# Sparse graph attention on one core: k and v rows of every batch stored in the original order by GpSimd, without a table of places

## The chip, the core and the metric

The kernel runs on one core of a Trainium2 chip. The metric is the device time of one execution in microseconds (us); three executions of the kernel before gave 1935.06, 1941.86 and 1942.67. One more execution was taken by the hardware profiler.

## What is computed

For 16 batches of 1024 rows with 512 numbers each, the reference is one layer of masked attention with eight heads, a residual and a normalisation of each row:

```
q, k, v = x @ Wq + bq, x @ Wk + bk, x @ Wv + bv      # 8 heads of 64
scores  = q . k / 8 + (1 - adj) * -1e9               # adj: 1024 x 1024, of 0 and 1
out     = softmax(scores) @ v
result  = layernorm(x + out @ Wo + bo)
```

The matrix adj is the same for all batches and is sparse: entry (i, j) is 1 with probability min(1, w_i w_j / 256), where w falls as one over the square root of the row number. Rows with a small number have up to some 80 keys, most have few, some none (such a row attends to all keys equally).

## The kernel before, in words

**Ranks.** The kernel sorts the rows by their number of keys, on the chip. `ranks` loads adj in eight tiles of 128 rows. For each, `most` (L382) counts the keys of each row on ScalarE (ACT), in place, and lets VectorE (DVE) multiply the tile by the column numbers and search the eight greatest, which are the row's last eight keys. From count and row number a key is made; TensorE (PE) spreads the keys over all partitions, and DVE compares each row's key with all others (L421), which gives its rank. GpSimd (POOL) scatters row number, count and keys by rank into a table `order` in device memory, and SP loads it back in sorted order as `ranked`; its first column, as integers, is `asked_row`: which row stands at each place of the sorted order. From then on x of batches 1 to 15 is gathered by POOL in sorted order, eight tiles of 128 rows a batch.

**Projections.** `transpose_x` and `pair` do a batch's tiles two by two: transposes, q, k and v (k and v of a pair by seven products of blocks in place of eight). k and v of 128 rows lie side by side in a tile `kv` of 128 x 1024 numbers (a pool of five buffers), and `send` stores it to `kv_rows`, a table of 1025 rows of 4 KB in device memory with three versions in turn (b % 3). q goes to `q_rows`. The last row of `kv_rows` serves queries without keys: zeros for k, the mean of all v.

**Attention by gathers.** A tile of 128 sorted queries works on blocks: block i is the i-th key of each of its queries, a gather of 128 rows from `kv_rows` by POOL (`gather`, L960). Seven tiles have 28 such blocks, and the two with most keys have six more, in which 128 edges are listed with their queries, which are gathered as well. So a batch has 34 blocks and 40 gathers for them. DVE multiplies q and k (`products`, L996) and adds by heads (`scores`), ACT takes the exponential, ACT or DVE weighs v, DVE adds up, or PE sums the edges.

**Row numbers.** Batch 0 is projected before the ranks are known, so its rows lie in the original order and the gathers use `key_row0`, the key's own number. The rows of later batches lie in sorted order, and the gathers use `key_row`, the key's place. The places come from a table `place_of`: seven small DVE operations (L438 to L443) turn ranks into places, SP stores 1024 numbers of 4 bytes (L444), and `places` (L475) has POOL fetch, 128 numbers at a time, the place of each key: 35 gathers.

**Order of the work.** The program is written out step by step: step n, from -39 to 543 and beyond, holds the exponentials of block n + 3, the products and scores of block n + 4, the gathers up to block n + 8, and a number of PE units (projections, output products) by a running credit. Each engine runs its own instructions in this order, so one that waits holds up all behind it on its engine. `later(k, ...)` puts a function k steps ahead. Steps below 0 are the lead-in: ranks, the projections of batch 0 and part of batch 1, and the lists of edges (`edges(7)` from step -24, `edges(6)` from step -9). Projections run one to two batches ahead of the attention.

**What the steps of the prediction touch.** DVE's column search is L384 and L385, the combinations T1 and T2 of the weights, which PE needs for its first seven-product pair, L333 and L334. `out_q` (L674) takes a buffer of the pool `q` of two; the tile `zero` (L305) is a third user of this pool. POOL's instructions of a batch are gathers of k and v (L986), of edge queries (L956), of x for the projections and for the residual (both L819, tiles `x` and `y`), the scatter of the result (L892), one gather of v (L966) and a power for each tile's variance (L880), whose result DVE uses two steps later (L883). SP stores kv (L692) and q, and loads q.

Of the kernel before, what the change touches and what calls it, by code (L numbers as in the profile page):

```python
# [10 lines left out]
F32 = mybir.dt.float32  # L11
# [31 lines left out]
ROWS = 3  # L43
# [11 lines left out]
PLACES_FROM = -22  # L55
# [112 lines left out]
def kernel(  # L168
# [75 lines left out]
    with ExitStack() as main:  # L244
# [34 lines left out]
        key_row, key_row0 = (one.tile([P, NS + NK], I32, name=name) for name in ("key_row", "key_row0"))  # L279
# [10 lines left out]
        place_row = one.tile([P, NT], I32, name="place_row")  # L290
        key, rank, moved = (one.tile([P, NT], F32, name=name) for name in ("key", "rank", "moved"))
# [7 lines left out]
        place_of = dram.tile([N + 1, 1], I32, name="place_of")  # L299
# [5 lines left out]
        zero = work.tile([1, D], F32, tag="q", name="zero", bufs=2)  # L305
        nc.gpsimd.memset(zero, 0.0)
# [5 lines left out]
        def loads():  # L312

            load_w(W["q"], wq)
            broadcast(bq_bc, bq)
            nc.vector.tensor_scalar(bq_bc, bq_bc, scale, None, op0=OP.mult)
            yield

            B12[0] = work.tile([P, 2, D], F32, tag="kv", name="b12", bufs=5)
            load_w(B11, wk[0:HD2, :])  # L320
            load_w(B21, wk[HD2:D, :])
            load_w(B12[0], wv[0:HD2, :])
            load_w(B22, wv[HD2:D, :])
            for _ in range(5):
                yield
            load_w(W["o"], wo)
            for i in range(ROWS):
                nc.scalar.dma_start(kv_rows[i][N:N + 1, 0:D], zero)
# [5 lines left out]
            nc.vector.tensor_tensor(T2, B22, T1, op=OP.subtract)  # L334
# [39 lines left out]
        def later(k, fn):  # L374
            plan.setdefault(now[0] + k, []).append(fn)
# [6 lines left out]
        def most(t, scratch):  # L382
            nc.scalar.activation(ADJ[t], ADJ[t], AF.Copy, accum_out=asked[:, t, 1:2])
            nc.vector.tensor_tensor(scratch, ADJ[t], place, op=OP.mult)  # L384
            nc.vector.max(out=asked[:, t, 2:], in_=scratch)  # L385

        def ranks():
# [6 lines left out]
            last_place = small.tile([1, 1], I32, name="last_place", bufs=1)  # L394
            nc.gpsimd.iota(last_place, pattern=[[1, 1]], base=N, channel_multiplier=0)
            nc.gpsimd.dma_start(place_of[N:N + 1, :], last_place)
            keys = work.tile([P, N], F32, tag="kv", name="keys", bufs=5)
            while now[0] <= max(ADJ_AT):
                for t in ADJ_AT.get(now[0], ()):
                    most(t, keys)  # L400
                yield
# [7 lines left out]
            row = work.tile([P, N], F32, tag="kv", name="key_of", bufs=5)  # L409
# [48 lines left out]
            for tiles, K in ((slice(0, short), SHORT_KEYS), *((slice(t, t + 1), OWN[t]) for t in range(short, NT))):  # L458
                n = tiles.stop - tiles.start
                rows, at = ranked[:, tiles, 2:2 + K], own[tiles.start]  # L460
                missing = absent[:, at:at + n * K].rearrange("p (t k) -> p t k", t=n)
                nc.vector.tensor_scalar(missing, rows, 0.0, None, op0=OP.is_lt)
                nc.vector.scalar_tensor_tensor(
                    key_row0[:, NS + at:NS + at + n * K].rearrange("p (t k) -> p t k", t=n), missing, NO_ROW, rows,
                    op0=OP.mult, op1=OP.max,
                )
            nc.vector.tensor_scalar(absent, absent, -NEG, None, op0=OP.mult)
            nc.vector.tensor_copy(key_row[:, NS:], key_row0[:, NS:])
# [28 lines left out]
        def edges(t):  # L497
# [60 lines left out]
            for i0 in range(0, nb, step):  # L558
# [19 lines left out]
                for rows in (key_row0, key_row):  # L578
                    nc.vector.tensor_tensor(rows[:, g0:g0 + n], e[:, 1, :], e[:, 0, :], op=OP.max)
# [12 lines left out]
            preps.append(places(range(first[t], first[t] + nb), 1))  # L592
# [72 lines left out]
        def pair(b, j):  # L665
# [8 lines left out]
            def out_q(i, p):  # L674

                assert gathered[0] >= NBT * (b - ROWS + 1)
                q = work.tile([P, D], F32, tag="q", name=f"q_{b}_{tt[i]}", bufs=2)
                nc.vector.scalar_tensor_tensor(q, p, scale, bq_bc, op0=OP.mult, op1=OP.add)
                later(1, lambda: nc.sync.dma_start(q_rows[b % ROWS][ds(tt[i] * P, P), :], q))
# [272 lines left out]
        def keys_of(b):  # L952
            return key_row if b else key_row0

# [5 lines left out]
        def gather(n):  # L960
            b, t, i = blocks[n]
            assert i < OWN[t] or t in listed
            if (t, i) == (ONE_KEY_AT[0], 0):
# [4 lines left out]
                    in_offset=bass.IndirectOffsetOnAxis(ap=keys_of(b)[:, g:g + 1], axis=0), element_offset=D,  # L968
# [10 lines left out]
            else:  # L979
# [8 lines left out]
                in_offset=bass.IndirectOffsetOnAxis(ap=keys_of(b)[:, g:g + 1], axis=0),  # L988
# [189 lines left out]
        prep.setdefault(PLACES_FROM, []).append(places([NS + own[t] + i for t in range(NT) for i in range(OWN[t])], 3))  # L1178
# [130 lines left out]
```

## Time and profile before

| | |
|---|---|
| three executions | 1935.06, 1941.86, 1942.67 us |
| profiled execution: its time | 1968.62 us |
| its span, first to last instruction | 1966.8 us |
| mean granted clock of PE | 0.984 of full speed |
| busy | PE 1874.8, DVE 1729.9, ACT 1549.2, POOL 1284.7 us |
| DMA | 541 MB in 185298 packets, 0.82 of 16 engines busy |
| PE busy in the first 165 us | 124.88 us |
| PE busy from 165 to 1500 us | 1325.55 of 1335 us |
| PE busy from 1500 us to the end | 424.33 of 467 us |

An engine's idle time is told with what ended it: "5.67 <-DVE t L334" means 5.67 us without work until the DVE instruction of line 334 that writes t was done. In groups of instructions the columns are line, engine, operation, tiles, form and count, then busy time and mean duration in ns of one, then the idle time before them. In tables by stretch each engine has its busy time and number of instructions; the last three columns are PE's granted clock, the busy share of the 16 DMA engines, and GB/s. POOL's durations are rough; its starts are not.

### The profile page before, as it was taken

The page shows a single profiled execution, that of the slowest core. Times are in us where ns is not written, and L with a number is a line of the kernel's source. Part 1 is how long each engine was busy: PE and PEld are TensorE (multiplying, and loading weights), DVE is VectorE, ACT ScalarE, POOL GpSimd, SP SyncE. Part 2 cuts the span into 40 slices and gives each one's busy share as a digit, 9 for nine tenths or more (in the row PEclk, how much of TensorE's full clock was granted, in tenths as well). Part 3 has the DMA queues.
Part 4 walks back from the last instruction along what each step waited for, and adds up shares of the span by engine and source line. Part 5 has one row for each costly group of instructions (what it writes and reads, how often), then busy time and mean ns, then how long its engine had stood idle before and what let it go on. Part 6 is the DMA issues. An engine that isn't in the chain of part 4 may idle for free.

```text
span 1966.8 us, 25244 instructions
## 1 busy us (share of the span) xinstructions
PE 1874.8 (95%) x5259; PEld 907.2 (46%) x5259; DVE 1729.9 (88%) x3506; ACT 1549.2 (79%) x6072; POOL 1284.7 (65%) x1201
## 2 busy tenths in 40 slices
PE   7959999999999999999999999999999999899996
PEld 3424444444545445454545445444544444344443
DVE  5658889999999998999998989989999898999894
ACT  3515777988888888888888888788879888989794
POOL 1455566777666676776777676666767676666684
PEclk9979999999999999999999999999999999999998
DMA  7427778898889888887988888887988889998983
GB/s 263 88 73 241 239 262 275 271 325 278 310 265 308 275 285 277 294 315 247 321 265 308 269 283 284 278 293 251 315 290 307 285 295 331 335 353 273 353 294 136
DMA packets 185298, 541.44 MB, mean 275 GB/s; under 512 B 32975, under 2 KB 32987, under 8 KB 185134
## 3 DMA queue, kind: packets, MB, share of 16 engines
q0 software_dynamic: 118736, 388.89, 60.4%
q1 hardware_dynamic: 63504, 145.33, 20.4%
q10 hardware_dynamic: 2894, 5.52, 0.8%
q14 instruction: 120, 0.98, 0.2%
q8 instruction: 44, 0.72, 0.1%
HBM read 423.95 MB, written 140.37 MB: 287 GB/s over the span
## 4 chain that ended last, share of the span: by engine, by line
PE 73%; DVE 11%; issue 4%; DMA 4%; ACT 2%; POOL 1%; another core or an unknown queue 1%; SPq 0%; POOLq 0%; DVEq 0%
PE po L648 19%; PE pq L648 15%; PE pp L765 12%; PE z L765 9%; PE x L765 8%; DVE qk L1007 2%; PE poT L1090 2%; PE pxT L615 2%; PE sum L1056 2%; PE sum L1057 2%; DVE s L1011 2%; ACT pv L1031 1%; DVE pv L1047 1%; DMA codes<-in_adj_dram,asked_row 1%; DMA kvg<-kv_rows,key_row 1%
## 5 line engine op out<-in xcount | busy, mean ns | idle before, releaser
L1031 ACT ACTIVATE pv<-kvg,pv 128x64 f32<-128x64 f32 x3544 | 892.5, 339 | 0.6 <-ACT pv L1021 0.6
L986 POOL DMA_INDIRECT kvg<-kv_rows,key_row x544 | 618.4, 1137 | 329.7 <-ACT pv L1031 96.8
L648 PE MATMUL po<-wo,oT 128*128 128x512 f32 x944 | 437.7, 597 | 2.0 <-DVE y L866 1.1
L648 PE MATMUL pq<-wq,xT 128*128 128x512 f32 x904 | 426.1, 601 | 1.0 <-DVE found L518 1.0
L1011 DVE TENSOR_REDUCE s<-qk 128x8 f32<-128x512 f32 x544 | 370.6, 681 | 7.4
L1007 DVE TENSOR_TENSOR qk<-qt,kvg 128x512 f32<-128x512 f32 x448 | 306.7, 684 | 9.3 <-DMA kvg<-kv_rows,key_row 8.6
L648 PEld LDWEIGHTS po<-wo,oT 128*128 128x128 f32 x944 | 177.7, 192 | 198.7 <-issue 188.3
L648 PEld LDWEIGHTS pq<-wq,xT 128*128 128x128 f32 x904 | 170.4, 193 | 198.3 <-issue 183.8
L765 PE MATMUL pp<-t,s 128*128 128x512 f32 x504 | 241.1, 602 | 12.2 <-DVE t L334 5.7
L765 PE MATMUL x<-b,xT 128*128 128x512 f32 x504 | 237.9, 595 | 0.0
L1047 DVE TENSOR_TENSOR pv<-pv,pv 128x520 f32<-128x520 f32 x336 | 233.4, 695 | 2.4 <-ACT pv L1031 1.7
L1021 ACT ACTIVATE pv<-s,absent 128x8 f32<-128x8 f32 x448 | 130.2, 293 | 69.7 <-DVE s L1011 53.3
L819 POOL DMA_INDIRECT x<-in_x_dram,asked_row x120 | 131.3, 1094 | 71.2 <-PE pxT L615 41.5
L892 POOL DMA_INDIRECT out_dram<-y,asked_row x128 | 151.5, 1183 | 37.9 <-issue 25.2
L658 ACT ACTIVATE sq_k<-kv 128x128 f32<-128x128 f32 x512 | 150.8, 300 | 13.8 <-issue 8.5
L765 PEld LDWEIGHTS pp<-t,s 128*128 128x128 f32 x504 | 95.5, 193 | 124.4 <-issue 116.6
L765 PEld LDWEIGHTS x<-b,xT 128*128 128x128 f32 x504 | 95.4, 191 | 114.0 <-issue 111.3
L956 POOL DMA_INDIRECT qg<-q_rows,query_row x96 | 106.3, 1108 | 51.0 <-issue 24.5
L765 PE MATMUL z<-b,s 128*128 128x512 f32 x252 | 122.8, 611 | 17.4 <-DVE kv L793 17.4
L819 POOL DMA_INDIRECT y<-in_x_dram,asked_row x102 | 115.1, 1129 | 30.7 <-issue 29.8
L765 PE MATMUL z<-t,s 128*128 128x512 f32 x252 | 119.8, 599 | 0.0
L765 PE MATMUL pp<-t,xT 128*128 128x512 f32 x252 | 118.5, 593 | 0.0
(208 smaller groups left out, 2582.0 us busy)
## 6 DMA issues: line engine op xcount, KB each, us to landing
kv_rows<-kv SPq DMA_DIRECT2D x128, 512.0 KB
q_rows<-q SPq DMA_DIRECT2D x113, 256.0 KB
qt<-q_rows SPq DMA_DIRECT2D x105, 256.0 KB
kvg<-kv_rows,key_row POOLq DMA_INDIRECT x544
residual<-x SPq DMA_DIRECT2D x26, 256.0 KB
y<-residual SPq DMA_DIRECT2D x26, 256.0 KB
adj<-in_adj_dram POOLq DMA_DIRECT2D x8, 512.0 KB
spill<-oT SPq DMA_DIRECT2D x10, 256.0 KB
```

Of the source, the lines that this page charges most:

```text
L648: nc.tensor.matmul(p, lhs(c), w[:, c, :], start=(c == 0), stop=(c == NPAIR - 1))
L658: nc.scalar.activation(sq, s[:, ts(h, P)], AF.Square, scale=scale, accum_out=sums[:, h:h + 1])
L765: nc.tensor.matmul(R[bank], l[:, ts(c, P)], right[:, c, :], start=(first and c == 0), stop=(c == 1), skip_group_check=True,)
L819: nc.gpsimd.indirect_dma_start(out=y, out_offset=None, in_=x_rows, in_offset=bass.IndirectOffsetOnAxis(ap=asked_row[:, t:t + 1], axis=0), ...
L892: nc.gpsimd.indirect_dma_start(out=out_rows[b, t], out_offset=bass.IndirectOffsetOnAxis(ap=asked_row[:, t:t + 1], axis=0), in_=y, in_offse ...
L956: nc.gpsimd.indirect_dma_start(out=q, out_offset=None, in_=q_rows[b % ROWS], in_offset=bass.IndirectOffsetOnAxis(ap=rows, axis=0))
L986: nc.gpsimd.indirect_dma_start(out=KG[n], out_offset=None, in_=kv_rows[b % ROWS], in_offset=bass.IndirectOffsetOnAxis(ap=keys_of(b)[:, g:g ...
L1007: nc.vector.tensor_tensor(QK[n], q, KG[n][:, 0:D], op=OP.mult)
L1011: nc.vector.tensor_reduce(S[n], QK.pop(n).rearrange("p (h d) -> p h d", d=HD), axis=AX.X, op=OP.add)
L1021: nc.scalar.activation(PV[n][:, D:], S.pop(n), AF.Exp, bias=bias)
L1031: nc.scalar.activation(pv[:, ts(h, HD)], v[:, ds(D + h * HD, HD)], AF.Copy, scale=pv[:, D + h:D + h + 1])
L1047: nc.vector.tensor_tensor(PV[b, t], PV[b, t], pv, op=OP.add)
```

## The change

The rows of `kv_rows` are kept in the original order in all batches. For batches 1 to 15 the tile kv, which holds rows in sorted order, is scattered by row number from POOL, two steps after it is ready instead of one, through eight views of `kv_rows` that are declared disjoint, so that the eight scatters of a batch do not wait for each other. Batch 0 is stored by SP as before. Keys need no translation: `key_row0`, `place_of`, `places`, its 35 gathers, the seven DVE operations and SP's store go.

In `most` DVE now reads the tile of adj as loaded, ahead of ACT, which writes its copy to another tile. The tile `zero` goes (the zeros come from `zeros`), and the first two q tiles of batch 0 take buffers of the pool `y` of six.

The core of the diff:

```diff
-        def most(t, scratch):
-            nc.scalar.activation(ADJ[t], ADJ[t], AF.Copy, accum_out=asked[:, t, 1:2])
+        def most(t, scratch, copied):
             nc.vector.tensor_tensor(scratch, ADJ[t], place, op=OP.mult)
             nc.vector.max(out=asked[:, t, 2:], in_=scratch)
+            nc.scalar.activation(copied, ADJ[t], AF.Copy, accum_out=asked[:, t, 1:2])
...
-            for at, by in ((LONE, LONE), (LONE + P, -LONE - P), (2 * P, P)):
-                nc.vector.tensor_scalar(key, rank, float(at), float(by), op0=OP.is_ge, op1=OP.mult)
-                if at == LONE:
-                    nc.vector.tensor_copy(moved, key)
-                else:
-                    nc.vector.tensor_tensor(moved, moved, key, op=OP.add)
-            nc.vector.tensor_tensor(place_row, rank, moved, op=OP.add)
-            nc.sync.dma_start(place_of[0:N, :].rearrange("(t p) o -> p (t o)", p=P), place_row)
...
-        def places(columns, per_step):
-
-            for i, g in enumerate(columns):
-                nc.gpsimd.indirect_dma_start(
-                    out=key_row[:, g:g + 1], out_offset=None, in_=place_of,
-                    in_offset=bass.IndirectOffsetOnAxis(ap=key_row0[:, g:g + 1], axis=0), bounds_check=N, oob_is_err=False,
-                )
-                if i % per_step == per_step - 1:
-                    yield
...
-                q = work.tile([P, D], F32, tag="q", name=f"q_{b}_{tt[i]}", bufs=2)
+                tag, bufs = ("q", 2) if b or j else ("y", Y_BUFS)
+                q = work.tile([P, D], F32, tag=tag, name=f"q_{b}_{tt[i]}", bufs=bufs)
...
             def send(i):
                 kv = KV[b, tt[i]]
-                later(1, lambda: nc.sync.dma_start(kv_rows[b % ROWS][ds(tt[i] * P, P), :], kv))
+                if b:
+                    later(2, lambda: nc.gpsimd.indirect_dma_start(
+                        out=kv_views[b % ROWS][tt[i]], out_offset=bass.IndirectOffsetOnAxis(ap=asked_row[:, tt[i]:tt[i] + 1], axis=0),
+                        in_=kv, in_offset=None,
+                    ))
+                else:
+                    later(1, lambda: nc.sync.dma_start(kv_rows[0][ds(tt[i] * P, P), :], kv))
...
-                in_offset=bass.IndirectOffsetOnAxis(ap=keys_of(b)[:, g:g + 1], axis=0),
+                in_offset=bass.IndirectOffsetOnAxis(ap=key_row[:, g:g + 1], axis=0),
```

More of the change, by code (lines that the diff above doesn't have):

```diff
@@ L54 @@
 REST_FROM = {7: -24, 6: -9}
-PLACES_FROM = -22
 PRODUCT = 0.86
@@ L278 @@
         sums = one.tile([P, NS, P], F32, name="sums")
-        key_row, key_row0 = (one.tile([P, NS + NK], I32, name=name) for name in ("key_row", "key_row0"))
+        key_row = one.tile([P, NS + NK], I32, name="key_row")
         query_row, query_row0 = (one.tile([P, NS], I32, name=name) for name in ("query_row", "query_row0"))
@@ L289 @@
         asked, ranked = (one.tile([P, NT, 2 + TOP], F32, name=name) for name in ("asked", "ranked"))
-        place_row = one.tile([P, NT], I32, name="place_row")
-        key, rank, moved = (one.tile([P, NT], F32, name=name) for name in ("key", "rank", "moved"))
+        key, rank = (one.tile([P, NT], F32, name=name) for name in ("key", "rank"))
         rank_row, asked_row = (one.tile([P, NT], I32, name=name) for name in ("rank_row", "asked_row"))
@@ L298 @@
         order = dram.tile([N, 2 + TOP], F32, name="order")
-        place_of = dram.tile([N + 1, 1], I32, name="place_of")
+        kv_views = [dram_disjoint_views(rows, NT) for rows in kv_rows]
         order_views = dram_disjoint_views(order, NT)
@@ L304 @@
         residual = [dram.tile([P, D], F32, name=f"residual_{i}") for i in range(B * NT - SPILL[0])]
-        zero = work.tile([1, D], F32, tag="q", name="zero", bufs=2)
-        nc.gpsimd.memset(zero, 0.0)
         zeros = work.tile([P, D + HEADS], F32, tag="pv0", name="zeros", bufs=3)
@@ L327, in loads @@
             for i in range(ROWS):
-                nc.scalar.dma_start(kv_rows[i][N:N + 1, 0:D], zero)
+                nc.scalar.dma_start(kv_rows[i][N:N + 1, 0:D], zeros[0:1, 0:D])
                 if i:
@@ L393, in ranks @@
             nc.vector.tensor_copy(asked[:, :, 0], query)
[L394 to L397, printed above, removed]
+            keys, row = (work.tile([P, N], F32, tag="kv", name=name, bufs=5) for name in ("keys", "key_of"))
             while now[0] <= max(ADJ_AT):
                 for t in ADJ_AT.get(now[0], ()):
-                    most(t, keys)
+                    most(t, keys, row)
                 yield
@@ L408, in ranks @@
                 nc.tensor.matmul(pk[t // 4][:, ts(t % 4, P)], keys[:, ts(t, P)], ident, start=True, stop=True)
-            row = work.tile([P, N], F32, tag="kv", name="key_of", bufs=5)
             for i in range(2):
@@ L463, in ranks @@
                 nc.vector.scalar_tensor_tensor(
-                    key_row0[:, NS + at:NS + at + n * K].rearrange("p (t k) -> p t k", t=n), missing, NO_ROW, rows,
+                    key_row[:, NS + at:NS + at + n * K].rearrange("p (t k) -> p t k", t=n), missing, NO_ROW, rows,
                     op0=OP.mult, op1=OP.max,
@@ L467, in ranks @@
             nc.vector.tensor_scalar(absent, absent, -NEG, None, op0=OP.mult)
-            nc.vector.tensor_copy(key_row[:, NS:], key_row0[:, NS:])
             for t in SHORT:
@@ L577, in edges @@
                 nc.vector.tensor_scalar(e[:, 0, :], e[:, 1, :], 0.0, NO_ROW, op0=OP.is_lt, op1=OP.mult)
-                for rows in (key_row0, key_row):
-                    nc.vector.tensor_tensor(rows[:, g0:g0 + n], e[:, 1, :], e[:, 0, :], op=OP.max)
+                nc.vector.tensor_tensor(key_row[:, g0:g0 + n], e[:, 1, :], e[:, 0, :], op=OP.max)
                 nc.vector.tensor_copy(query_row[:, g0:g0 + n], g[:, :, J + 2])
@@ L591, in edges @@
             listed.add(t)
-            preps.append(places(range(first[t], first[t] + nb), 1))
         X, XT, SX, KV, VSUM, NRM, Y, OT, PS = {}, {}, {}, {}, {}, {}, {}, {}, {}
@@ L950 @@
         blocks = [(b, t, i) for b in range(B) for t in range(NT) if t != ONE_KEY for i in range(OWN[t] + BLOCKS[t])]
-        def keys_of(b):
-            return key_row if b else key_row0
         def gather_q(q, b, rows):
@@ L967, in gather @@
                     out=V1[b], out_offset=None, in_=kv_rows[b % ROWS],
-                    in_offset=bass.IndirectOffsetOnAxis(ap=keys_of(b)[:, g:g + 1], axis=0), element_offset=D,
+                    in_offset=bass.IndirectOffsetOnAxis(ap=key_row[:, g:g + 1], axis=0), element_offset=D,
                 )
@@ L1177 @@
         prep.setdefault(CHECKS_AT, []).append(checks())
-        prep.setdefault(PLACES_FROM, []).append(places([NS + own[t] + i for t in range(NT) for i in range(OWN[t])], 3))
         preps = [loads(), ranks()]
```

## The prediction, made before the changed kernel was run

> **What bounds the kernel now.** I read the busy times and the chain of waits first, then tables by stretch, then POOL's groups where the store is added, and the lead-in instruction by instruction.
>
> ```profile
> PE 1874.8 (95%) x5259; PEld 907.2 (46%) x5259; DVE 1729.9 (88%) x3506; ACT 1549.2 (79%) x6072; POOL 1284.7 (65%) x1201
> ...
> PE 73%; DVE 11%; issue 4%; DMA 4%; ACT 2%; POOL 1%; another core or an unknown queue 1%; SPq 0%; POOLq 0%; DVEq 0%
> ```
>
> PE is the bound, and POOL hardly stands on the chain. By stretch:
>
> ```profile
> 300.00:1500.00 1200.00, 1190.75 (x3383) 579.76 (x3382) 1109.81 (x2206) 1012.91 (x4027) 837.33 (x776) 1.00 0.85 287
> 77.00:82.00 5.00, 4.98 (x12) 2.01 (x11) 4.68 (x25) 4.93 (x15) 3.06 (x4) 1.00 1.51 63
> 82.00:87.00 5.00, 5.00 (x13) 2.28 (x12) 1.08 (x3) 4.93 (x7) 0.81 (x1) 1.00 0.71 27
> 87.00:92.00 5.00, 5.00 (x13) 2.21 (x12) 0.00 (x0) 1.23 (x3) 3.01 (x3) 1.00 1.00 370
> 105.00:132.00 27.00, 13.83 (x24) 5.20 (x23) 9.19 (x29) 1.07 (x8) 19.09 (x20) 0.75 0.16 42
> ```
>
> Read three things. In mid-run PE lacks 9 us of 1200, so nothing can be won there, only lost. From 77 to 87 the DMA engines are occupied (1.51, 0.71) but move 63 and 27 GB/s. From 105 to 132 PE, DVE and ACT do little, though the DMA engines are nearly idle. POOL in mid-run:
>
> ```profile
> L986 POOL DMA_INDIRECT kvg<-kv_rows,key_row x364 | 411.2, 1130 | 200.1 <-issue 63.2 <-ACT pv L1031 59.5 <-ACT pv L1021 29.3
> L892 POOL DMA_INDIRECT out_dram<-y,asked_row x85 | 100.5, 1183 | 26.0 <-issue 17.3 <-ACT pv L1031 3.4 <-ACT pv L1021 2.3
> ```
>
> 364 gathers at 34 a batch are 10.7 batches, 112 us each. The lead-in, DVE then PE:
>
> ```profile
> 22.86 0.69 DVE L678 SCALAR_TENSOR_TENSOR q<-pq,bq_bc 128x512 f32<-128x512 f32 x1 [6.95 <-DMA q_rows<-q]
> 92.49 1.23 DVE L506 TENSOR_TENSOR codes<-codes,place 128x1024 f32<-128x1024 f32 x1 [9.37 <-DMA codes<-in_adj_dram,asked_row]
> ```
>
> ```profile
> 42.70 3.75 PE L765 MATMUL pp<-t,s 128*128 128x512 f32 x4 [5.67 <-DVE t L334]
> 103.16 1.12 PE L615 MATMUL pxT<-ident,x 128*128 128x128 f32 x4 [6.37 <-DVE w L781]
> 121.52 3.78 PE L765 MATMUL z<-b,s 128*128 128x512 f32 x4 [8.01 <-DVE kv L793]
> 132.03 3.75 PE L765 MATMUL pp<-t,s 128*128 128x512 f32 x4 [4.19 <-remote]
> ```
>
> Each PE wait is a loss to the whole, since PE is full from 165 to 1500.
>
> **The skill.** (1) The Trainium skill, DMA: Bandwidth & Descriptors, Specifications: under 512 B the DMA engines read, modify and write. SP's store of places is 1024 elements of 4 B, issued at 75.84; the slow stretch 77 to 87 follows at once, so the trace agrees in effect. (2) Same page, "Issuing engines are not separate DMA queues": issuing elsewhere only shifts the issuer's time. The trace agrees on the shift: an SP issue of a kv store takes 0.32 us (median), a POOL scatter 1.18. (3) TensorE: Matmul & The Clock Gate, Part 1: after idling PE runs at half clock for a while. The trace agrees: four products take 3.75 us at 42.70 and 1.88 at 50.71. (4) GPSIMD Engine Reference, Key points: POOL shares its SBUF interface with DVE. The x gather takes 0.95 us at 80.61, with little on DVE, and 1.11 on average in mid-run, which fits.
>
> **The change part by part.**
>
> *Pool of q and search.* DVE's second q waited 6.95 us for the first one's store, as `zero` held the other buffer. Its product was done at 18.45 (PE's timeline), so with buffers of its own it starts 4.4 us earlier, and the search behind it too: DVE did sixteen operations of 1.23 us without a wait, so the search never waited for ACT, and that edit is worth nothing beside this one. Were ACT ever late, it would cost what ACT is late by. T1 and T2 follow the search, so PE's 5.67 shrinks by 4.4, and the half clock behind it goes too: 3.75 - 1.88 = 1.9 us on that group, and 1.0 on the next (4.63 for eight, where 3.60 is usual). Sum -7.3.
>
> *The table's store.* Without it the codes (issued 78.02, landed 92.5) should arrive within some 7 us, as do gathers in mid-run. DVE then does not stand 9.37 us, and PE's 6.37 goes, with the half clock behind it (z at 104.07 takes 3.02 in place of 1.88): -7.5. If the slow stretch had another cause, 0. The seven DVE operations (0.16 to 0.22 us each) lie in a stretch where PE is full: nothing.
>
> *35 gathers of places.* 35 x (1.05 + 0.30) = 47 us of POOL, on which nothing waits but later gathers with slack: nothing by themselves. But from 105 to 132 they are nearly all that POOL does, and waits of 1 to 2 us stand between dependent DVE operations which take 0.1 us before. PE loses 8.0 + 4.2 + 1.0 (at 108.09) and, by half clock, 1.9 + 0.9 + 1.9 on the groups at 121.52, 125.09 and 132.03: 17.9. If the gathers cause this, it goes. Does it exist in unprofiled runs? The profiled run is 26.8 us longer than the median, and PE cannot be that much fuller in mid-run, so I take it that most of that stretch belongs to the profiled run. Bounds 0 and -18; I take 0 for the median, -18 for the profile.
>
> *120 scatters on POOL.* Nearest rows: the result's scatter 1.18, k and v gathers (the same 4 KB rows) 1.13, plus 0.30 between POOL's DMAs: 1.48; bounds 1.25 (quiet 0.95) and 1.8 (rows of 1.5 occur). Mid-run: POOL is busy 837 us, 690 DMAs leave 0.30 each, 207; 156 of 1200 are free, 14.6 a batch. Eight scatters take 11.8. POOL goes from 87% to 97% of the batch. The free time is badly placed: from 729 to 750, round a batch's start, POOL runs 16 instructions without a wait. Walking through its timeline, adding 1.43 at each of SP's stores and taking off every wait over 0.30, leaves 3 to 5 us of backlog at the first product of batches 2 to 12. There a gather is issued only 6 to 9 us ahead of its product (13 to 15 in the middle of a batch), and the two that came late at 740.9 and 743.9 needed 7 to 8. So DVE stands some 3 us a batch. PE covers about 2: those two waits (2.9 us) left PE busy 111.00 of 111 us. Left: 1 us. Queued behind POOL's scatter are also the powers; a quarter end within 5.6 us of DVE's use, a twentieth within 1.6: I add 0.6. Sum 1.6 x 13 batches = +21. Bounds 0 and the rival below.
>
> *Waits of the scatter.* Its kv tile is two steps old, and the rows that it overwrites were gathered half a batch before: 0. On SP the stores go, which hurts nobody; SP's store of the mean now waits for POOL's last scatter, with 13 us of slack for the q loads behind it: 0. On the DMA queues 63 MB move from q1 (20.4% for 145 MB) to q0 (60.4% for 389): 18 us of 16 engines over the run, 1% of their time: inside the 21.
>
> Sum on the profiled execution: 1968.6 - 7.3 - 7.5 - 17.9 + 21 = 1957. On the median, 26.8 us lower: 1941.9 - 14.8 + 21 = **1948**.
>
> **Rivals.** *Lead-in wins:* the stretch 105 to 132 is in every run, and POOL absorbs half: 1941.9 - 33 + 11 = 1920. For it: the stretch coincides with the gathers. Against: from 93 to 104 the same gathers do no harm. *POOL becomes the bound:* of POOL's waits, those for the variance (27.5 us in mid-run) and for x's buffers (23.9) stay, 4.8 a batch, since they come from positions in the program, not from earliness. Then a batch takes 97.5 + 11.8 + 4.8 = 114.1 with scatters of 1.48 and 116.7 with 1.8; middle +3.3 x 13 = 43: 1941.9 - 15 + 43 = 1970. It decides from where scatters and remaining waits exceed 14.6 us a batch. Against: a late POOL finds such waits over. *Not what it says:* the same rows are gathered from another order, so fewer or other rows are not read; dropped.
>
> **Numbers.** Mine (1934 to 1961) 40%, lead-in wins (1905 to 1932) 27%, POOL bound (1955 to 1990) 33%. A difference under 0.5% (9.7 us) this measurement can't tell from none. Faster 27% (the first rival), same 25% (most of mine), slower 48% (the rest of mine, the second rival). Range 1914 to 1980; mine alone 1934 to 1961.
>
> **What would show it.** Right: DVE's second q near 18.5, no stretch with full engines at 30 GB/s after 77, codes within 8 us, POOL's waits in mid-run near 30 us, DVE's waits for kvg up from 7 to some 35 us, PE lacking some 25 us from 300 to 1500. Wrong: PE as full as before (then -15 or more is kept), or a batch of 114 us and more with POOL hardly waiting.

## The result, and the profile after

The changed kernel takes 1944.82 us (median of 20; 1938.97 to 1948.64), the kernel before 1939.05 us (median of 20; 1935.06 to 1943.72). The ratio is 1.0026, with an interval of 1.0017 to 1.0035: 5.8 us slower, where the forecast had 6.1. The profiled execution of the changed kernel took 1947.77 us (span 1946.0) and that of the kernel before 1968.62 us, so the two profiles differ the other way round; where that comes from is a main question below.

First the busy times and the chain of waits of the changed kernel:

```profile
PE 1872.7 (96%) x5259; PEld 905.5 (47%) x5259; DVE 1730.4 (89%) x3496; ACT 1550.5 (80%) x6072; POOL 1380.3 (71%) x1283
...
PE 73%; DVE 10%; DMA 5%; issue 3%; ACT 2%; POOL 1%; SPq 0%; POOLq 0%; DVEq 0%; ACTq 0%
```

POOL has 82 more instructions (120 scatters added, 35 gathers and three others gone) and 96 us more work; PE's work is the same. By stretch, in the columns told of above:

```profile
300.00:1500.00 1200.00, 1184.97 (x3354) 574.68 (x3353) 1103.44 (x2189) 1010.02 (x4014) 925.89 (x856) 1.00 0.85 285
77.00:82.00 5.00, 5.00 (x13) 2.13 (x12) 4.70 (x14) 4.96 (x13) 0.00 (x0) 1.00 0.60 225
82.00:87.00 5.00, 5.00 (x13) 2.24 (x12) 4.65 (x18) 0.21 (x2) 0.00 (x0) 1.00 0.28 108
87.00:92.00 5.00, 5.00 (x19) 2.68 (x18) 4.61 (x20) 2.83 (x11) 1.90 (x2) 1.00 0.13 27
105.00:132.00 27.00, 20.93 (x64) 9.71 (x65) 20.66 (x51) 7.78 (x31) 13.27 (x13) 0.94 0.61 195
```

Two things are to be seen. In mid-run PE lacks 15.0 us of 1200 where it lacked 9.3, and it gets through 29 matmuls fewer (3354 for 3383), which at 0.352 us each are 10 us: 5.8 of them are the longer waits, the rest is that a matmul takes 0.353 us on average. In the lead-in the DMA engines are no longer occupied without moving bytes: at 77 to 82 a share of 0.60 moves 225 GB/s, where 1.51 moved 63. From 105 to 132 PE works 20.93 us in place of 13.83, and DVE 20.66 in place of 9.19.

POOL's groups in mid-run, 300 to 1500 us:

```profile
L961 POOL DMA_INDIRECT kvg<-kv_rows,key_row x359 | 407.9, 1136 | 122.9 <-issue 57.8 <-ACT pv L1006 17.1 <-DVE pv L1010 10.2
L870 POOL DMA_INDIRECT out_dram<-y,asked_row x85 | 96.0, 1130 | 24.8 <-issue 14.7 <-ACT pv L996 2.6 <-ACT sq_k L629 1.2
L665 POOL DMA_INDIRECT kv_rows<-kv,asked_row x82 | 94.9, 1157 | 23.1 <-issue 16.5 <-DVE qk L982 2.4 <-DVE vsum L684 0.9
```

A scatter takes 1.157 us, and the idle time ahead of POOL's gathers has gone from 200 to 123 us: POOL used its waits up. DVE's side of it, from the table of waits of the same stretch (time waited, number, longest):

```profile
DVE qk L982 <- DMA kvg<-kv_rows,key_row: 20.8, 19, 4.2
```

The same line in the kernel before:

```profile
DVE qk L1007 <- DMA kvg<-kv_rows,key_row: 6.9, 5, 1.7
```

In the lead-in, DVE's second q and the codes, and the only two waits of PE from 30 to 150 us:

```profile
17.79 0.69 DVE L650 SCALAR_TENSOR_TENSOR q<-pq,bq_bc 128x512 f32<-128x512 f32 x1 [2.74 <-PE pq L619]
...
77.05 1.22 DVE L479 TENSOR_TENSOR codes<-codes,place 128x1024 f32<-128x1024 f32 x1 [1.02 <-DMA codes<-in_adj_dram,asked_row]
```

```profile
108.32 0.59 PE L514 MATMUL poff<-est,before 128*128 128x1 f32 x2 [3.86 <-DVE est L511]
131.83 5.40 PE L362 MATMUL pb<-wo,bvb 128*128 128x512 f32 x8 [2.75 <-DVE bvb L358]
```

All four waits of PE shown of before are gone. DVE's first product of batch 0 starts at 132 us, where it was 164, and the first of batch 15 at 1823, where it was 1842. So in these two profiled executions the lead-in got 32 us shorter, 15 batches took 1691 us in place of 1678, 13 more, and the end 1.5 less.

### The profile page after: what moved, and what is told of

Read it like the earlier page. It is cut to its first block, busy times and chain, and to the rows that moved or that the text cites. A ratio compares the mean times of both kernels' runs of the same rounds, so it can differ in the third digit from the quotient of the medians.

```text
span 1946.0 us, 25024 instructions
## 1 busy us (share of the span) xinstructions
PE 1872.7 (96%) x5259; PEld 905.5 (47%) x5259; DVE 1730.4 (89%) x3496; ACT 1550.5 (80%) x6072; POOL 1380.3 (71%) x1283
## 3 DMA queue, kind: packets, MB, share of 16 engines
q1 hardware_dynamic: 45184, 82.41, 11.8%
## 4 chain that ended last, share of the span: by engine, by line
PE 73%; DVE 10%; DMA 5%; issue 3%; ACT 2%; POOL 1%; SPq 0%; POOLq 0%; DVEq 0%; ACTq 0%
PE po L619 18%; PE pq L619 16%; PE pp L743 13%; PE z L743 9%; PE x L743 9%; DMA kvg<-kv_rows,key_row 2%; DVE qk L982 2%; PE poT L1065 2%; PE pxT L586 2%; DVE s L986 2%; PE sum L1032 2%; PE sum L1031 1%; ACT pv L1006 1%; DVE pv L1022 1%; PE pm L688 1%
## 5 line engine op out<-in xcount | busy, mean ns | idle before, releaser
L743 PE MATMUL pp<-t,s 128*128 128x512 f32 x504 | 237.1, 593 | 0.5 <-DVE s L605 0.5
L870 POOL DMA_INDIRECT out_dram<-y,asked_row x128 | 144.9, 1132 | 36.5 <-issue 21.4
L665 POOL DMA_INDIRECT kv_rows<-kv,asked_row x120 | 138.9, 1158 | 35.1 <-issue 20.9
L797 POOL DMA_INDIRECT y<-in_x_dram,asked_row x102 | 108.8, 1066 | 32.3 <-issue 30.2
```

What stands on the lines that cost most here:

```text
L665: later(2, lambda: nc.gpsimd.indirect_dma_start(out=kv_views[b % ROWS][tt[i]], out_offset=bass.IndirectOffsetOnAxis(ap=asked_row[:, tt[i]: ...
L743: nc.tensor.matmul(R[bank], l[:, ts(c, P)], right[:, c, :], start=(first and c == 0), stop=(c == 1), skip_group_check=True,)
L797: nc.gpsimd.indirect_dma_start(out=y, out_offset=None, in_=x_rows, in_offset=bass.IndirectOffsetOnAxis(ap=asked_row[:, t:t + 1], axis=0), ...
L870: nc.gpsimd.indirect_dma_start(out=out_rows[b, t], out_offset=bass.IndirectOffsetOnAxis(ap=asked_row[:, t:t + 1], axis=0), in_=y, in_offse ...
```

## The experiments

The experiments form three series of four kernels, each series on one chip, beside runs of the kernel before. The three chips are different ones; which chip gave the result above is not on record. The same program differs by up to 3% between the four occasions: the kernel before took 1939, 1968, 1995 and 1971 us (medians). So kernels are compared within a series.

**First series: which part of the table of places costs (kernel before 1967.76 us, 27 runs).** The search and pool edits alone, put into the kernel before:

```diff
-                q = work.tile([P, D], F32, tag="q", name=f"q_{b}_{tt[i]}", bufs=2)
+                tag, bufs = ("q", 2) if b or j else ("y", Y_BUFS)
+                q = work.tile([P, D], F32, tag=tag, name=f"q_{b}_{tt[i]}", bufs=bufs)
...
-            nc.scalar.activation(ADJ[t], ADJ[t], AF.Copy, accum_out=asked[:, t, 1:2])
...
+            nc.scalar.activation(copied, ADJ[t], AF.Copy, accum_out=asked[:, t, 1:2])
```

> The kernel before with one part of the change: the two first q tiles in the pool y, no tile zero, DVE's search ahead of ScalarE; the table of places stays. Theory of the prediction: DVE's second q starts 4.4 us earlier and PE's wait for T1 and T2 nearly goes, so -7 us on the median (1932) and the same on the profile. Rival (the lead-in gives little in unprofiled runs, because what the search gains is waited for later, at the codes of the edges): 0 to -3 us. The profile also tells whether the stretch in which all engines stand, from 105 to 132 us, comes again with the gathers of places: if it belongs to them, yes; if it was an accident of one execution, no.

Measured: 1964.54 us (22 runs), ratio 0.9977 (0.9960 to 0.9994). The edit does what it was said to do to DVE, 18.20 in place of 22.86 in its timeline, and the waits of the table stay. The first two come 6 to 7 us earlier, the last hardly (at 120.89, where it was 121.52), and PE's wait at 105.47 is longer than the 1.0 us that stood there before:

```profile
18.20 0.69 DVE L676 SCALAR_TENSOR_TENSOR q<-pq,bq_bc 128x512 f32<-128x512 f32 x1 [2.74 <-PE pq L645]
```

```profile
85.47 1.23 DVE L503 TENSOR_TENSOR codes<-codes,place 128x1024 f32<-128x1024 f32 x1 [9.22 <-DMA codes<-in_adj_dram,asked_row]
```

```profile
96.89 1.11 PE L612 MATMUL pxT<-ident,x 128*128 128x128 f32 x4 [7.13 <-DVE vsum L704]
105.47 5.27 PE L645 MATMUL pq<-wq,xT 128*128 128x512 f32 x8 [4.05 <-DVE found L515]
120.89 3.78 PE L763 MATMUL z<-b,s 128*128 128x512 f32 x4 [8.43 <-DVE kl L522]
```

3 us came, and the first product of batch 0 is 4 us earlier (160): no more than the 4.7 us by which DVE's second q is earlier, and less than the 7 of the codes. The stretch from 105 to 132 came again with the gathers of places, on another occasion than that of the profile of before:

```profile
105.00:132.00 27.00, 17.60 (x30) 7.03 (x30) 11.94 (x32) 0.75 (x2) 13.85 (x14) 0.75 0.18 49
```

The changed kernel with all stores of k and v by SP:

```diff
-                if b:
-                    later(2, lambda: nc.gpsimd.indirect_dma_start(
...
-                else:
-                    later(1, lambda: nc.sync.dma_start(kv_rows[0][ds(tt[i] * P, P), :], kv))
+                later(1, lambda: nc.sync.dma_start(kv_rows[b % ROWS][ds(tt[i] * P, P), :], kv))
```

> The changed kernel with the k and v rows of all batches stored by SP as before, in sorted order, while the gathers use the keys' own row numbers: wrong rows are gathered from batch 1 on, as many and as large. It has the whole lead-in of the change and nothing of its cost in mid-run. Theory of the prediction: the lead-in is worth 15 us and the scatters cost 21, so 1924 beside 1939 before and 1945 after. Rival (both were put too high by the same amount): 1932 to 1935, lead-in worth 4 to 7 and scatters 10 to 13.

Measured: 1933.74 us (6 runs), ratio 0.9830 (0.9806 to 0.9854).

The kernel before without SP's store of places and without the 35 gathers:

```diff
-            nc.sync.dma_start(place_of[0:N, :].rearrange("(t p) o -> p (t o)", p=P), place_row)
...
-            preps.append(places(range(first[t], first[t] + nb), 1))
...
-        prep.setdefault(PLACES_FROM, []).append(places([NS + own[t] + i for t in range(NT) for i in range(OWN[t])], 3))
```

> The kernel before without the store of the table of places and without its 35 gathers; the keys' own numbers are used in all batches, so wrong rows are gathered from batch 1 on, as many and as large. Theory of the prediction: the store of 4-byte elements is worth 7.5 us, the gathers nothing in unprofiled runs: -7.5 on the median. Rival (lead-in wins): -25. Rival (the table lies beside other work): 0 to -2.

Measured: 1940.19 us (6 runs), ratio 0.9859 (0.9832 to 0.9886): 28 us. Its codes are used at 81.29 with a wait of 0.91 us, PE is busy 144.80 us of the first 165 where it was 124.88, and the stretch from 105 to 132, on the same chip as the one just shown, is:

```profile
105.00:132.00 27.00, 23.19 (x67) 10.40 (x66) 19.31 (x53) 8.14 (x35) 8.90 (x9) 0.87 0.47 152
```

With the 3 us of the search this makes 31 of the 34 us that the kernel with SP's stores gains. So on this chip the 33 us that the prediction found in the profile, and took as 15 for the median, are there in runs without the profiler, if not how they divide between the store and the gathers.

One gather of 40 bytes a row for each tile of k and v, unread, added to the kernel with SP's stores:

```diff
+                            out=few, out_offset=None, in_=order, in_offset=bass.IndirectOffsetOnAxis(ap=asked_row[:, tt[i]:tt[i] + 1], axis=0)
...
```

> As the kernel with the stores on SP, and in the place of each scatter POOL issues a gather of 128 x 40 bytes that nobody reads: POOL's time of the scatters without their bytes in its DMA queue, and without their waits. If POOL's time is what costs (theory of the prediction), it takes nearly as long as the changed kernel: 1942 to 1945. If the rows' bytes in front of the gathers in POOL's DMA queue cost, it is as quick as the kernel with the stores on SP, within 3 us.

Measured: 1988.27 us (6 runs), ratio 1.0102 (1.0063 to 1.0140): with 120 small gathers the kernel takes 54.5 us more than with SP's stores alone, 0.45 us for each. That is more than either expectation, and not by late gathers of k and v: the first six of batches 2 to 12 are issued 10.1 us ahead of their products, 11.1 with SP's stores. In places every engine stands. After the small gather issued at 941.17, from the timeline of all engines:

```profile
941.17 0.99 POOL L668 DMA_INDIRECT few<-order,asked_row  x1 [0.17 <-issue]
...
951.40 1.07 ACT L590 COPY xT<-pxT 128x512 f32<-128x512 f32 x2 [5.21 <-remote]
951.52 0.69 DVE L773 TENSOR_TENSOR kv<-z,g 128x512 f32<-128x512 f32 x1 [1.53 <-remote]
951.63 0.94 POOL L799 DMA_INDIRECT x<-in_x_dram,asked_row  x1 [1.47 <-remote]
952.04 1.12 PE L1067 MATMUL poT<-ident,v 128*128 128x128 f32 x4 [5.56 <-issue]
```

All four go on within 0.7 us of each other, and none waits for an instruction that had only just ended: "remote" and "issue" are waits whose releaser the profile doesn't find. This doesn't show that the small gather is the cause: in the kernel without powers of the second series, which has no small gather, the same instructions stand at the same place of the program, ACT for 5.36 us until 958.24, POOL for 1.70 until 958.48, PE for 4.30 until 958.88.

**Second series: the changed kernel again, the form of the table, POOL's time (kernel before 1995.34 us, 59 runs).** The changed kernel itself:

> The changed kernel itself, once more beside the kernel before, since in the first series of experiments the kernel before took 1968 us (27 executions, 1961 to 1979) where it had taken 1939 (20 executions, 1935 to 1944) beside the changed kernel. Theory: the stretch in which all engines stand belongs to the small gathers of places and is there on some chips, or in some states of a chip, and not in others; so the changed kernel, which has none, takes about 1945 wherever it runs, and the kernel before 1939 or 1967. Rival: the whole chip is slower there, then both are slower by the same 1.5 per cent.

Measured: 2004.63 us (22 runs), ratio 1.0045 (1.0024 to 1.0066). From 300 to 1500 us:

```profile
300.00:1500.00 1200.00, 1152.91 (x3232) 556.40 (x3231) 1060.97 (x2104) 970.22 (x3841) 894.78 (x823) 0.99 0.82 274
```

So a chip on which the kernel before is slow does not make the change a gain; the mid-run pays there too.

The kernel before with its table stored as 8 rows of 512 bytes, after one transpose on PE, in place of 1024 numbers of 4 bytes:

```diff
-            nc.vector.tensor_tensor(place_row, rank, moved, op=OP.add)
-            nc.sync.dma_start(place_of[0:N, :].rearrange("(t p) o -> p (t o)", p=P), place_row)
+            nc.vector.tensor_tensor(moved, rank, moved, op=OP.add)
+            pp_ = fill_psum("pplaces")
+            nc.tensor.transpose(pp_[0:NT, 0:P], moved, ident)
+            nc.vector.tensor_copy(place_t, pp_[0:NT, 0:P])
+            nc.sync.dma_start(place_of[0:N, :].rearrange("(t p) o -> t (p o)", p=P), place_t)
```

> The kernel before, with the places turned by TensorE first, so that the table is stored as 8 rows of 512 bytes and not as 1024 elements of 4; the gathers of places stay. If the 4-byte store makes the slow stretch of the DMA engines from 77 to 87 us (theory of the prediction), the stretch goes, the codes of the edges land within 8 us of their issue in place of 14.4, and the median falls by up to 7.5 us. Rival (the stretch is the burst of stores that waited in SP's queue): 14 us as before, and no gain.

Measured: 1974.63 us (6 runs), ratio 0.9898 (0.9861 to 0.9934), 21 us. The codes land by 83.17, 5.8 us after their issue, where it was 14.4; DVE's wait for them is gone, as is the stretch of occupied DMA engines (PE has a new wait of 4.20 us, for the input of the transpose), while 105 to 132 is still poor:

```profile
86.38 1.22 DVE L509 TENSOR_TENSOR codes<-codes,place 128x1024 f32<-128x1024 f32 x1
```

```profile
77.00:82.00 5.00, 5.00 (x16) 2.35 (x15) 2.56 (x17) 1.99 (x3) 1.97 (x2) 1.00 0.93 292
82.00:87.00 5.00, 5.00 (x16) 2.46 (x15) 3.07 (x7) 4.97 (x14) 3.72 (x4) 1.00 0.69 236
105.00:132.00 27.00, 18.63 (x36) 7.28 (x36) 21.40 (x61) 4.59 (x20) 17.93 (x18) 0.83 0.29 95
```

So the store's 4-byte form was what made the codes late. What is left at 105 to 132 stands beside the gathers of places, which this kernel keeps.

POOL kept busy in the places of the scatters, but by six memsets of a scratch tile for each tile of k and v, SP storing:

```diff
+                        for _ in range(6):
+                            nc.gpsimd.memset(idle, 0.0)
...
```

> As the kernel with the stores on SP (its gathers use the wrong rows from batch 1 on), and in the place of each scatter POOL fills a scratch tile six times, some 1.5 us: POOL's time of a scatter without any DMA. The kernel with the stores on SP took 1934. If POOL's time is the cost of the scatters, this one takes what the changed kernel takes, 10 us more; if their bytes in the queue cost, no more than 3 us more. It also tells whether the small gathers of the run before cost 54 us as POOL's time (then this one takes about 1985) or as small gathers (then it does not).

Measured: 1987.92 us (22 runs), ratio 0.9965 (0.9948 to 0.9981): 17 us under the changed kernel of this series. The kernel with SP's stores was not in it, so what the memsets cost can't be read here.

The changed kernel with POOL's powers taken off it (a copy on DVE in their place, so the rows are not scaled rightly):

```diff
-                    nc.gpsimd.tensor_tensor(st[:, 3:4], st[:, 2:3], neg_half, op=OP.pow)
+                    nc.vector.tensor_copy(st[:, 3:4], st[:, 2:3])
...
```

> The changed kernel with the powers of the variances left out: DVE copies the variance in the power's place, so the output is not normalised rightly. POOL is relieved of 0.67 us and a short gap eight times a batch, 7 us of the 11.6 that the scatters add. If POOL's lateness at a batch's start costs the 11 us in mid-run, more than half comes back: 1937 to 1940 where the changed kernel takes 1945. If not, no gain over 2 us.

Measured: 2012.12 us (22 runs), ratio 1.0061 (1.0034 to 1.0087), no better than the changed kernel. POOL is busy 830.04 us of 1200 in place of 894.78, the first six gathers of batches 2 to 12 are early again (11.4 us ahead in place of 9.4), and DVE waits for gathers 3.2 us in place of 14.0, yet PE stays as low, and DVE has other waits:

```profile
300.00:1500.00 1200.00, 1153.73 (x3239) 556.72 (x3239) 1067.72 (x2192) 973.44 (x3856) 830.04 (x742) 0.99 0.82 275
...
DVE y L844 <- remote: 10.0, 4, 4.1
...
DVE kv L771 <- remote: 6.2, 2, 6.0
DVE kv L766 <- remote: 5.7, 2, 3.6
```

The copies give DVE 7 us more work in these 1200. Unless they alone ate up what POOL's relief brought, which no run separates, POOL's lateness is not what costs most on this chip.

**Third series: all terms on one chip (kernel before 1970.69 us, 43 runs).** The changed kernel, the same with SP's stores, and the one with memsets were run together, and a fourth: the kernel before with the table by rows, the search edits of the first series, and its gathers of places issued one a step:

```diff
-        prep.setdefault(PLACES_FROM, []).append(places([NS + own[t] + i for t in range(NT) for i in range(OWN[t])], 3))
+        prep.setdefault(PLACES_FROM, []).append(places([NS + own[t] + i for t in range(NT) for i in range(OWN[t])], 1))
```

> The changed kernel once more, as the common base for the three kernels beside it on this chip. The size of its difference from the kernel before has come out as +5.8 and +9 us so far: +0.2 to +0.6% expected here. If the theory holds that the table's cost depends on the occasion (a stretch in which all engines stand near 105 us, worth up to 28 us, present on some chips and not on others), a chip on which the kernel before is fast (near 1940) shows it slower by about 0.3%, and one on which the kernel before has the stretch (1968 and more) shows it at the most equal or faster by up to 1%, unless its own scatters stall there too.

> The changed kernel with all stores of k and v by SP, one step after they are ready, into rows by position (so from batch 1 on the gathers read other rows of the same size: the output isn't the reference's). Same lead-in as the changed kernel, no scatters on POOL: the difference to the changed kernel on this chip is the scatter's whole cost. The prediction has 21 us (1.6 us a batch). If POOL becomes the bound it is 40 or more; if the scatters were free and the cost lay elsewhere, under 5. Mid-run, 300 to 1500 us: POOL busy near 825, against 895 to 926 with scatters.

> The kernel with all stores of k and v by SP (wrong rows from batch 1 on: the output isn't the reference's), and POOL occupied for about 1.5 us by six memsets of a scratch tile wherever the changed kernel has a scatter: POOL's time without the DMA. If the cost of the scatters is POOL's occupation (gathers issued later at a batch's start), the time is that of the changed kernel within 6 us. If it is what the scatters do on the DMA queues or at the receiving end, the time is that of the kernel with SP's stores within 6 us.

> The kernel before, with the table of places kept, and three edits: the changed kernel's pool of q and column search; the table stored as 8 rows of 512 bytes after one transpose on PE; the gathers of places issued one a step in place of three. Keeps SP's stores of k and v. Theory: the table cost what it did by the form of its store and by the bunching of its gathers, not by being there, so this should have both the better lead-in and the unhurt mid-run: 15 to 30 us under the kernel before and 15 to 35 under the changed one (-0.8 to -1.5%). Rival: the small gathers cost wherever they stand, each some 0.5 to 1 us in all engines; then spreading them moves the loss into the projections of batch 1 and wins nothing over the store by rows alone, some -10 to -20 us under the kernel before.

| kernel | median us | ratio to before (interval) | first product of batch 0 | from there to batch 15 |
|---|---|---|---|---|
| before (its one profile, another occasion) | 1970.69 | 1 | 164 | 1678 |
| changed | 1979.92 (22 runs) | 1.0033 (1.0015 to 1.0051) | 131 | 1730 |
| changed, SP stores | 1936.66 (6 runs) | 0.9807 (0.9772 to 0.9842) | 131 | 1678 |
| SP stores, POOL busy by memsets | 1981.29 (21 runs) | 1.0051 (1.0037 to 1.0065) | 131 | 1728 |
| before, table by rows, search, spread | 1955.42 (6 runs) | 0.9905 (0.9873 to 0.9937) | 133 | 1697 |

The sum can be read off: without table and without scatters the kernel is 34.0 us faster than before, all of it ahead of the first product (as far as the one profile of before, from another occasion, can tell); the scatters give back 43.3 us, all of it after. Tables by stretch of the changed kernel, of that with SP's stores, and of that with memsets, in this order:

```profile
0.00:165.00 165.00, 148.15 (x410) 69.75 (x411) 129.33 (x292) 81.59 (x256) 54.97 (x66) 0.98 0.59 199
300.00:1500.00 1200.00, 1167.21 (x3277) 563.84 (x3276) 1077.95 (x2138) 986.26 (x3914) 902.34 (x837) 0.99 0.83 278
```

```profile
0.00:165.00 165.00, 148.22 (x412) 69.86 (x413) 129.46 (x292) 81.74 (x257) 50.89 (x62) 0.98 0.58 199
300.00:1500.00 1200.00, 1187.27 (x3374) 576.96 (x3373) 1106.03 (x2195) 1011.38 (x4014) 836.30 (x783) 1.00 0.85 288
```

```profile
0.00:165.00 165.00, 149.06 (x405) 69.93 (x406) 128.06 (x289) 79.91 (x249) 56.18 (x85) 0.97 0.57 198
300.00:1500.00 1200.00, 1161.18 (x3270) 561.92 (x3269) 1074.03 (x2132) 984.20 (x3901) 956.03 (x1235) 0.99 0.82 278
```

With scatters PE gets through 97 matmuls fewer in these 1200 us than with SP's stores, 34 us of work at 0.352 us each. Its longer waits are 20 us of that; the other 14 are the clock, granted at 0.99 in place of 1.00, so that a matmul takes 0.356 us on average. The clock was low in six stretches, 30.7 us together (3.4 with SP's stores), and each began during a wait of PE of 1.9 us or more, or at most 1.4 us after its end. So an idle PE loses more than the time for which it stands idle.

Memsets and scatters end within 1.4 us of each other here (the memsets were 17 us better in the second series). By the measure of the expectation the cost would be POOL's occupation. But they don't get there by the same waits. With memsets DVE waits for gathers; with scatters a quarter of that, and 13.2 us in three waits for a releaser that the profile doesn't find (tables of DVE's waits in the same stretch, memsets first):

```profile
DVE qk L983 <- DMA kvg<-kv_rows,key_row: 39.4, 23, 5.4
```

```profile
DVE y L844 <- remote: 13.2, 3, 8.4
DVE qk L982 <- DMA kvg<-kv_rows,key_row: 10.4, 10, 3.0
```

The memsets are also the heavier load: 480 of them hold POOL for 150 us of these 1200, where 82 scatters hold it for 93 and leave gaps of 0.30 between (25). So they show that POOL's time alone can cost this much, not that it is what costs it here. That it has a part is likely: the first six gathers of batches 2 to 12 are issued 8.8 us ahead of their products with scatters, 7.5 with memsets and 10.3 with SP's stores.

What "remote" is can be seen in the longest of these waits. From DVE's timeline:

```profile
492.50 0.16 DVE L976 TENSOR_REDUCE lone_norm<-lone 128x1 f32<-128x4 f32 x1 [0.56 <-remote]
501.07 0.69 DVE L844 TENSOR_TENSOR y<-po,y 128x512 f32<-128x512 f32 x1 [8.41 <-remote]
```

The product po that it waits for left PE at 491.80. The trace's semaphore events tell the rest:

```
PE's instructions that raise its semaphore, ends:  491.80 492.65 495.25 496.12 497.84 498.28
the same semaphore's six changes:                  501.05 501.09 501.18 501.24 501.30 501.36
```

Six changes, due over 6.5 us, all come within 0.3 us, the oldest 9.3 us late; ACT's next instruction waits on the same semaphore and starts at 501.20, and PE then waits for DVE. Three scatters, two of k and v and one of the result, had been issued at 487.76, 489.10 and 490.38. The Trainium skill (Perfetto Trace Analysis, Per-engine timelines) says that the time a semaphore update takes to spread is not part of an instruction in the profile; this case agrees in that the changes come after the ends. Whether all of the 9 us is spreading, the profile can't tell, since the ends of PE's instructions are modelled in it. I counted waits of over 0.8 us on an engine's semaphore that was changed more than 0.8 us after its last instruction had ended, from 300 to 1500 us: DVE 26.0 and ACT 31.2 us in the changed kernel, 14.3 and 21.8 with SP's stores, 10.1 and 15.9 with memsets. Of DVE's 26.0 us all, and of ACT's 31.2 us 24.2, are on PE's semaphore. In the profile of the first occasion's changed kernel there is none. But the scatters are not needed for such waits: the kernel with its table by rows in the second series, which has none, has 37.1 and 37.5 us of them, the changed kernel beside it 27.2 and 26.1, though PE lacks 26 us there and 47 in the changed kernel.

The fourth kernel shows that gathers of places cost where they are put. By stretch:

```profile
105.00:132.00 27.00, 24.65 (x76) 11.21 (x74) 23.43 (x57) 9.63 (x40) 15.19 (x16) 1.00 0.59 195
132.00:165.00 33.00, 21.48 (x50) 9.52 (x51) 18.17 (x49) 12.02 (x50) 23.58 (x23) 0.79 0.53 156
```

105 to 132 is full now, but 132 to 165 has 21.48 us of PE where the changed kernel had 32.87 in its first profile, and batch 0 takes 142 us in place of 127 to 131 in the others. It is 15 us under before and 24 under the changed kernel: the lower end of what the theory expected, and within the rival's.

## Why the prediction was right

**The total**: +6.1 us forecast on the median, +5.8 measured, for a sum of a gain and a loss, as it said. The prediction held a difference of under 9.7 us to be too small to tell from none; the 20 runs of each kernel tell this one. Both terms were of the right kind. That their sum came out is in part luck. On the third chip, where both were measured, the gain was 34.0 us (forecast 14.8) and the loss 43.3 (forecast 21): both terms were too small by a factor of two, and the errors cancel (+9.2). On the first occasion the two were never measured apart, so whether their sizes were right there is not known.

**Pool and search, -7.3**: too large. DVE's second q came at 17.79 (forecast 18.5), and PE's 5.67 us at 42.70 went. But put alone into the kernel before, the edit brought 3.2 us (1.2 to 7.9 by the interval). The waits that the table causes lie behind it and stayed: 9.22 for the codes, 8.43 for PE. The half clock that was added is not seen in the time.

**Table's store, -7.5**: right in cause, low in size. The codes landed within 6 us of their issue (71.10 to 77.05), the stretch from 77 went, and with the store by rows PE's wait of 6.37 us was gone. It brought 21 us on its chip, and the first product of batch 0 came 13 us earlier (151). The chips differ, so the size beyond 13 isn't certain.

**35 gathers of places, -18 on the profile and 0 on the median**: this is the step that failed. I took the stretch from 105 to 132 to belong to the profiled run, because that was 26.8 us longer than the median. It doesn't belong to the profiler: beside the experiments, the kernel before took 1960.77 us or more in each of 129 executions, none as short as on the first occasion, the stretch came again in the profile with the search edits, and leaving out the table is worth 28 us in runs without a profile. It belongs to the chip or the occasion. The profile's 1968.62 us lie among the runs of the first series (1960.77 to 1979.25) and outside the 20 of the result, so it seems that three runs of one occasion and a profile of another were compared as if they were one population. What the gathers alone are worth was not measured, as no run leaves them out and keeps the store. The store by rows brought 21 us on one chip and the whole table 28 on another, which would leave 7; on the third chip the kernel that keeps the gathers, one a step, takes 18.8 us more than the one with SP's stores. How DVE stood there is seen in its timeline, kernel before:

```profile
111.63 0.28 DVE L519 SCALAR_TENSOR_TENSOR codes<-codes,found 128x64 f32<-128x64 f32 x1 [1.78 <-remote]
112.33 0.23 DVE L520 MAX8 found<-codes 128x8 f32<-128x64 f32 x1 [0.41 <-DVE codes L519]
```

and in the changed kernel, where the same operations follow each other:

```profile
80.35 0.28 DVE L492 SCALAR_TENSOR_TENSOR codes<-codes,found 128x64 f32<-128x64 f32 x1
80.67 0.23 DVE L493 MAX8 found<-codes 128x8 f32<-128x64 f32 x1
```

DVE waited for its own semaphore while small gathers ran: the search ahead of the line at 111.63 ended at 109.84, and its change came at 111.61, 1.8 us late. That is a late change as in mid-run, and here no end is modelled. The first rival's lead-in (-33) was right on these chips (-34.0). On the first occasion the parts were not measured apart; the kernel before at 1939 leaves little room for all of it, as no kernel was under 1926 in any run. If the 13 us that mid-run lost in the profile is what it lost in the median, the lead-in gave about 7 there. That is worked out, not shown.

**120 scatters, +21**: the mechanism was seen as forecast in the first occasion's profile. A scatter takes 1.157 us (forecast 1.18); what POOL's waits have beyond 0.30 us each fell from 156 to 48 in 1200 us (forecast near 30); the first six gathers of batches 2 to 12 are issued 7.3 us ahead of their products, where it was 10.0; DVE's waits for gathers rose to 20.8 (forecast 35), and PE lacked 15.0 (forecast 25). The cost was 13 us over the run, 8 below. One profile is thin ground for that: the kernel with SP's stores, without scatters, took 1692 us from the first product to batch 15 in its profile of the first series, which was 14 us longer than the median of that kernel. The half clock, which the prediction priced in the lead-in, it left out in mid-run, where the lower clock made 14 of the 34 us that PE lost on the third chip. On the third chip it was 43.3, the second rival's number, but not its mechanism: that rival has POOL hardly waiting, and POOL there still waits 75 us of 1200; in the second series relieving POOL of 65 us brought nothing. What is larger there than with SP's stores is both DVE's waits for gathers (10.4 us, where they are 2.5) and the late semaphore changes.

**Two readings.** The two late gathers, used at 740.9 and 743.9, took 7.2 and 8.9 us from issue to use, not 7 to 8. The example for the interface that POOL shares with DVE was badly chosen: around 80.61 DVE was busy too, 4.68 of the 5 us from 77 to 82. In mid-run of the same profile the reading holds: the 16 x gathers beside which DVE worked less than 60% of the time took 0.98 us on average, the 43 beside which it never paused 1.20.

**The rivals.** "Lead-in wins" was right in the lead-in, and wrong that POOL absorbs half. "POOL becomes the bound" had the size of the loss on the slower chips, but POOL isn't the bound there. Either alone would have been off by 25 us.

**Open.** What delays a semaphore's change, and why on three occasions and not in the changed kernel's profile of the first. It is seen beside small gathers in the lead-in and beside scatters of k and v in mid-run, but also in the mid-run of kernels that have neither there, and no run took it away while leaving the DMAs. So the cause of the 43 us is not shown. Three loads in the place of the scatters cost about as much each, over SP's stores: scatters 43.3 us, memsets 44.6, small gathers 54.5 in another series. What they share is 1.4 us or more of POOL's time a tile; what they don't share is late gathers. How the loss divides between late gathers and late changes is open too: the table of DVE's waits gives 10.4 us to the first, and the rest was not apportioned.

## What to carry to other kernels

Before a stretch of a profile is written off as belonging to that one run, compare the run with others on its own chip; here the kernel before differed by 56 us between occasions, ten times the effect, while the ratio of the changed kernel beside it held to 1.0026 to 1.0045. Price a moved store by the room its engine has where others depend on its being early: POOL had 14.6 us free a batch and the scatters needed 11.8, and the move still cost 43 us where it was measured. Count the clock that PE loses after a wait beside the wait itself: 14 us beside 20 in mid-run of the third series. And write small tables as whole rows: 8 rows of 512 bytes in place of 1024 numbers of 4 bytes brought 21 us.

## What the runs showed of the hardware that was not expected

- Semaphore changes can come late, several at once, and every engine that waits on them stands: six of PE's came up to 9.3 us after the ends that the profile models, one of DVE's own 1.8 us after its measured end. The profile names such waits "remote" or "issue".
- 120 gathers of 128 rows of 40 bytes, read by nobody, cost 54.5 us, where 120 scatters of 128 rows of 4 KB cost 43.3 us in another series, and memsets that move nothing by DMA 44.6 beside these. What the loads cost did not follow their bytes.
- The same program took 1939, 1968, 1971 and 1995 us on four occasions, with every run within 1% of its median.
